# The edge table by exclusive-or and minimum, two groups of x instead of six, and the whole choice ahead of slots and running maxima

## The chip, the cores and the metric

The kernel runs on one core of one Trainium2 chip. The metric is device microseconds of one execution. The core has five engines that run side by side, each in its own program order: TensorE (PE in the profile; its weight loads are PEld), VectorE (DVE), ScalarE (ACT), GpSimd (POOL) and SyncE (SP). SP, ACT and POOL also issue DMA transfers; the gathers, whose row addresses lie in SBUF, are issued by POOL.

## The reference

The input is a graph: x has 6250 nodes of 256 features, and there are 100000 edges, sorted by their target node dst. Each node gets the maximum, over its incoming edges, of a linear map of both ends; then it is added to x and normalised.

```python
x_src = x[src]
x_dst = x[dst]
theta_x = (x_dst - x_src) @ theta_w.T + theta_b
phi_x = x_src @ phi_w.T + phi_b
e = jax.nn.relu(theta_x + phi_x)
out = jax.ops.segment_max(e, dst, num_segments=x.shape[0])
out = jnp.where(jnp.isfinite(out), out, 0.0)
x = _layernorm(x + out, axis=-1)
```

The part of an edge that depends on its source is b = x (phi_w - theta_w)^T, the rest depends on the target alone. So a node needs the maximum of the rows b[src] over its edges, and the target's own part is added afterwards.

## The kernel before

The first part of the nodes (1130) and the second (5120, 40 on each of 128 partitions) get their maxima in different ways.

**b.** All 49 row tiles of x (128 rows each) are loaded (x_q), transposed on TensorE (L746), copied by ScalarE (L748), multiplied by the weights (L758), copied again (L761) and stored to the DRAM tensor b_rows (L779). This is `b_of`.

**The first part.** Its edges lie 146 to a partition (`T1`), in 19 groups of 8 steps. A step is one gather of 128 rows by POOL (L512) into a tile of a ring of six (`gathered`, the tile g), and then one running maximum on VectorE (L688), each over the one before; a group's maxima are stored to maxima_1. A group that is gathered before b exists takes rows of x, and `x_group` runs `b_of` over them in place: `X_GROUPS` = 6 groups go this way, the rest gather from b_rows. Behind each gather, while `paced[0]` is 2, POOL runs two small iotas into a tile named pause.

**The second part** has two ways. For up to 24 edges of each node (`CHOICE_R`) nothing is gathered. The sources are cut into 17 slots of 383 nodes. For each slot, each node chooses one edge whose source lies in it (`choice`, nine batches of two slots, L1003 to L1021); the choice is transposed and sent to DRAM (`wanted`, chosen_rows). A part of the fetch (`slot_part`: one slot, 1024 nodes, 85 parts in all) loads the chosen rows' numbers (want, L1065), makes three blocks of one-hot columns from them (hot: two ScalarE instructions a block, L1071 and L1072, or, from the list on, one of VectorE, L1069, for the first of three blocks), and multiplies the slot's rows of b, split into a high and a low half (terms, L1057 and L1058), by them (L1079). VectorE takes the maximum into acc (L1090); for slot 0 ScalarE copies instead (L1088). The edges that no slot took form the list: `list_pieces` packs them on VectorE in 16 pieces (the moves are L1204 and L1207), sends them through DRAM, gathers them back in three long gathers (`gather_run`), and then 29 groups of 8 steps are gathered from b_rows by list_src and run as in the first part.

**The edge table** (`fill_table`) brings the edges of a partition's 40 nodes, up to 800 of them, from where they lie in order to a table of 40 x 36 places. Each word holds the distance that it has still to move, times WORD, and above zero its source; ten rounds (steps 512, 256, ... 1) move those whose bit is set. A round is three VectorE instructions: the moved words (L966), the words that stay (L969), and their sum (L972), between two tables in turn. A word of zero is an empty place.

**What sets the order.** A scheduler orders each engine's instructions by the order in the source and its own costs; `behind_in_order` pins one instruction behind another without a wait on the chip. `in_turn` keeps POOL's gathers in the order of the source, and each run's step is pinned behind a gather of the next group. In the list stage VectorE's runs are pinned behind the latest part's maximum (`latest_part`).

The order of the source is: gathers of x for six groups; b, with the first x group behind the seventh share and the others at the end; the table; nine times a choice, its `wanted` and `next_group_1(1)`; the list pieces, of which some carry `next_group_1(1)` and every other of the rest one part; what is left of the first part; the list's 29 groups, with the parts that are left spread over them; the closing shares (L1283 to L1348), which gather the maxima, add, normalise and store.

```python
def next_group_1(n):
    if groups_1:
        i = groups_1.pop(0)
        gathers = gather_group(i, b_rows)
        if i > X_GROUPS:
            run_1(i - 1, gathers)
    if todo:
        node_place(todo.pop(0))
    fetch_parts(n)
```

## Time and profile before

| what | us |
|---|---|
| median of three runs | 744.11 (743.1 to 745.2) |
| profiled execution, its time | 744.23 |
| its span on the core | 742.4 |
| TensorE busy | 655.6 |
| VectorE busy | 636.6 |
| ScalarE busy | 507.7 |
| GpSimd busy | 515.8 |

The profile is one execution. A group's row gives the source line, engine, operation, output and input tiles with their shapes, how often, the busy time in us with the mean of one in ns, and after the bar the time the engine was idle just before them, with what ended it. A row by stage gives start and end of a stretch, its length, the busy time of each engine with the number of its instructions, the clock granted to TensorE, the busy share of the DMA engines and GB/s. A row in order of time gives start, length, and what ran.

### The profile page before, as it was taken

The page shows a single profiled execution, that of the slowest core. Times are in us where ns is not written, and L with a number is a line of the kernel's source. Part 1 is how long each engine was busy: PE and PEld are TensorE (multiplying, and loading weights), DVE is VectorE, ACT ScalarE, POOL GpSimd, SP SyncE. Part 2 cuts the span into 40 slices and gives each one's busy share as a digit, 9 for nine tenths or more (in the row PEclk, how much of TensorE's full clock was granted, in tenths as well). Part 3 has the DMA queues.
Part 4 walks back from the last instruction along what each step waited for, and adds up shares of the span by engine and source line. Part 5 has one row for each costly group of instructions (what it writes and reads, how often), then busy time and mean ns, then how long its engine had stood idle before and what let it go on. Part 6 is the DMA issues. An engine that isn't in the chain of part 4 may idle for free.

```text
span 742.4 us, 10003 instructions
## 1 busy us (share of the span) xinstructions
PE 655.6 (88%) x3018; PEld 540.4 (73%) x3018; DVE 636.6 (86%) x1213; ACT 507.7 (68%) x714; POOL 515.8 (69%) x561
## 2 busy tenths in 40 slices
PE   0599998998875998899999999999999999789943
PEld 0388787886664866688888888888888888579943
DVE  6499999999987988498979888889888989968874
ACT  0144446969995797688778777877877776037882
POOL 7598987888987777777777777777767364037710
PEclk9999999999997899999999999999999999999986
DMA  7476756576477678988787878778867676336652
GB/s 219 135 254 207 274 192 221 167 255 205 139 228 231 215 215 300 300 295 271 235 264 221 283 250 248 242 240 284 269 209 244 186 255 208 137 107 192 206 200 76
DMA packets 56470, 164.83 MB, mean 222 GB/s; under 512 B 11899, under 2 KB 19860, under 8 KB 49332
## 3 DMA queue, kind: packets, MB, share of 16 engines
q1 hardware_dynamic: 32920, 98.76, 38.5%
q0 software_dynamic: 20944, 57.62, 27.3%
q10 hardware_dynamic: 2540, 7.69, 2.8%
q8 instruction: 27, 0.44, 0.3%
q14 instruction: 39, 0.32, 0.1%
HBM read 101.08 MB, written 63.74 MB: 222 GB/s over the span
## 4 chain that ended last, share of the span: by engine, by line
PE 49%; DVE 8%; POOL 7%; DMA 6%; ACT 6%; issue 4%; SPq 0%; DVEq 0%; ACTq 0%; POOLq 0%
PE ps_f L1079 45%; POOL g L512 6%; DMA g<-b_rows,src 4%; DMA want<-chosen_rows 2%; ACT x_f L1348 2%; ACT squares L1333 2%; PE ps_e L1303 2%; DVE acc L1090 2%; DVE g L688 1%; ACT x_t L1298 1%; DVE g L1314 1%; DVE x_f L1318 1%; PE ps_e L1296 1%; DVE work L1176 0%; POOL dst_w L512 0%
## 5 line engine op out<-in xcount | busy, mean ns | idle before, releaser
L1079 PE MATMUL ps_f<-hot,terms 128*128 128x512 f32 x1960 | 463.6, 397 | 30.7 <-DVE acc L1090 15.2
L1079 PEld LDWEIGHTS ps_f<-hot,terms 128*128 128x128 f32 x1960 | 371.9, 191 | 118.5 <-DVE acc L1090 18.5
L512 POOL DMA_INDIRECT g<-b_rows,list_src x232 | 233.2, 1005 | 84.6 <-issue 61.1
L1071 ACT ACTIVATE hot<-want,minus_row 128x1024 fp32r<-128x1024 f16 x179 | 197.4, 1146 | 82.6 <-PE ps_f L1079 72.6
L1090 DVE TENSOR_TENSOR acc<-acc,ps_f 128x1024 f32<-128x1024 f32 x160 | 193.4, 1215 | 30.5 <-PE ps_f L1079 29.6
L688 DVE SCALAR_TENSOR_TENSOR g<-g,caps 128x256 f32<-128x256 f32 x376 | 180.3, 479 | 15.2 <-DMA g<-b_rows,src 11.7
L1072 ACT ACTIVATE hot<-hot 128x1024 fp32r<-128x1024 f32 x179 | 179.5, 1047 | 0.0
L512 POOL DMA_INDIRECT g<-b_rows,src x98 | 130.4, 1330 | 30.0 <-issue 25.9
L758 PE MATMUL ps_b<-weights,x_t 128*128 128x256 f32 x388 | 92.4, 393 | 5.1 <-ACT x_t L748 4.5
L758 PEld LDWEIGHTS ps_b<-weights,x_t 128*128 128x128 f32 x388 | 74.0, 196 | 19.1 <-ACT x_t L748 9.3
L512 POOL DMA_INDIRECT g<-maxima,place x49 | 47.1, 962 | 54.6 <-DVE g L1315 29.2
L512 POOL DMA_INDIRECT g<-in_x_dram,src x48 | 62.5, 1302 | 11.6 <-issue 6.6
L1069 DVE TENSOR_SCALAR hot<-want,row_id 128x1024 fp32r<-128x1024 f16 x66 | 50.4, 766 | 6.7 <-DMA want<-chosen_rows 6.7
L1303 PE MATMUL ps_e<-weights,x_t 128*128 128x256 f32 x192 | 49.4, 386 | 0.2 <-ACT x_t L1298 0.2
L1303 PEld LDWEIGHTS ps_e<-weights,x_t 128*128 128x128 f32 x192 | 33.6, 195 | 3.8 <-ACT x_t L1298 0.5
L761 ACT COPY b_sb<-ps_b 128x512 f32<-128x512 f32 (+1 forms) x25 | 14.5, 578 | 29.1 <-PE ps_b L758 29.1
L1298 ACT COPY x_t<-ps_e 128x512 f32<-128x512 f32 x24 | 13.7, 575 | 29.6 <-PE ps_e L1296 29.6
L488 POOL IOTA pause<- 128x160 f32 x102 | 29.9, 293 | 3.4
L748 ACT COPY x_t<-ps_xt 128x512 f32<-128x512 f32 (+1 forms) x49 | 26.4, 594 | 6.1 <-PE ps_xt L746 5.9
L1333 ACT ACTIVATE squares<-x_f,r 128x256 bf16<-128x256 f32 x49 | 24.3, 500 | 7.7 <-DVE r L1330 7.7
L1348 ACT ACTIVATE x_f<-x_f,r 128x256 f32<-128x256 f32 x41 | 21.5, 591 | 9.2 <-DVE r L1340 9.1
L761 ACT COPY g<-ps_b 128x512 f32<-128x512 f32 x24 | 14.1, 589 | 17.8 <-PE ps_b L758 16.7
(267 smaller groups left out, 500.2 us busy)
## 6 DMA issues: line engine op xcount, KB each, us to landing
maxima<-g SPq DMA_DIRECT2D x47, 1024.0 KB
want<-chosen_rows SPq DMA_DIRECT2D x85, 256.0 KB
x_q<-in_x_dram SPq DMA_DIRECT2D x12, 512.0 KB
b_rows<-b_sb ACTq DMA_DIRECT2D x12, 512.0 KB
raw<-b_rows SPq DMA_DIRECT2D x16, 256.0 KB
x_f<-in_x_dram SPq DMA_DIRECT2D x4, 1024.0 KB
out_dram<-x_f SPq DMA_DIRECT2D x4, 1024.0 KB
g<-b_rows,list_src POOLq DMA_INDIRECT x232, 3.9
```

Source lines behind the costliest of these rows:

```text
L488: return nc.gpsimd.iota(t, pattern=[[step, t.shape[1]]], base=base, channel_multiplier=per_partition, allow_small_or_imprecise_dtypes=True,)
L512: in_turn(nc.gpsimd.indirect_dma_start(out=out, out_offset=out_offset, in_=in_, in_offset=in_offset))
L688: one = nc.vector.scalar_tensor_tensor(g[:, k, :], last[part], caps[:, t : t + 1], g[:, k, :], op0=ALU.min, op1=ALU.max)
L758: nc.tensor.matmul(ps[:, h, :], x_t[:, h, k, :], weights[:, k, 0, :], start=(k == 0), stop=(k == KC - 1))
L1069: nc.vector.tensor_scalar(hot[:, b, :], want, row_id[:, b : b + 1], None, op0=ALU.is_equal)
L1071: nc.scalar.activation(hot[:, b, :], want, AF.Abs, bias=minus_row[:, b : b + 1], scale=1.0)
L1072: nc.scalar.activation(hot[:, b, :], hot[:, b, :].bitcast(FP), AF.Relu, bias=1.0, scale=-1.0)
L1079: nc.tensor.matmul(ps[:, w : w + 512], terms[:, part, b, h * P : (h + 1) * P], hot[:, b, w : w + 512], start=(i == 0), stop=(i == n - 1),)
L1090: latest_part[0] = nc.vector.tensor_tensor(to, to, ps, op=ALU.max).ins.name
L1303: nc.tensor.matmul(a[:, i, :], x_t[:, 2 * i + c, :], weights[:, c, 1, :], start=(c == 0), stop=False)
L1333: nc.scalar.activation(squares, x_f[:, k, :], AF.Square, bias=mean[:, k : k + 1], scale=1.0, accum_out=var[:, k : k + 1])
L1348: nc.scalar.activation(x_f[:, k, :], x_f[:, k, :], AF.Identity, bias=mean[:, k : k + 1], scale=inv[:, k : k + 1])
```

## The change

- X_GROUPS goes from 6 to 2. Sixteen steps gather from x, the other 130 of the first part from b_rows. The two x groups get their `b_of` behind all shares, and their runs stand in the source behind the choices. The pauses behind the early gathers are gone.
- In the table, a word is a float between 2^23 and 2^24, whose low bits hold the source and above it the distance; an empty place is 2^100. A round is one exclusive-or with the step's bit on the words' bits, and one minimum into the same table: a word whose bit is set becomes smaller by it where it should go, and one whose bit isn't set becomes larger. The slot code is worked out after the spreading, over the whole table (`floor_of` on 1440 columns), instead of before it on 800. The list takes its sources out of the word by one mask.
- All nine choices come first; then two parts, the runs of the two x groups, and the list's 16 pieces, each with a `next_group_1` of one or two parts in turn. Eighteen gathers of the first part now stand on POOL behind the list's three long ones.
- `ahead_of_run` pins: slot 0's subtraction (L1058) behind the last choice, and the first running maximum of each first-part group behind the latest choice or list move. The memset of raw is pinned behind the table's words.

```diff
 FIRST_STEPS = 146
-X_GROUPS = 6
+X_GROUPS = 2
 TILES = 40
...
 CHOICE_R = 24
-X_AFTER = 6
-WORD = 8720
+WORD = 1 << 13
 TABLE_BITS = 10
...
 LOWEST = -1.0e30
-ABSENT = 1 << 14
+EMPTY = 2.0**100
+FAR_OFF = 2.0**30
 MAGIC = 12582912.0
...
     latest = [None]
-    paced = [2]
+    paced = [0]
...
     latest_part = [None]
+    ahead_of_run = [None]
...
                     behind_in_order(one, gathers[k], "rows that are there")
+                if part == 1 and k == 0 and ahead_of_run[0] is not None:
+                    behind_in_order(one, ahead_of_run[0], "choice and list ahead of the first part")
                 if part == 2 and latest_part[0] is not None:
...
                 b_of(rows, rows)
-            run_1(i)
-
-        for k, share in enumerate(shares(4)):
+
+        for share in shares(4):
             n = share[2]
...
             nc.scalar.dma_start(node_rows(b_rows, *share), present(b_sb, *share))
-            if k == X_AFTER:
-                x_group(of_x[0])
-        for i in of_x[1:]:
+        for i in of_x:
             x_group(i)
...
         source, w_3 = work_2[:, :W], work_1[:, TR - W :]
-        iota(w_3, 1, TR - W + 1, 0)
-        nc.vector.memset(words[:, : TR - W], 0.0)
-        nc.vector.memset(work_1[:, : TR - W], 0.0)
-        nc.vector.tensor_scalar(local, dst_w, first_node, None, op0=ALU.subtract)
+        iota(w_3, 1, TR - W + 1 + R // 2, 0)
+        nc.vector.memset(words[:, : TR - W], EMPTY)
+        nc.vector.tensor_scalar(local, dst_w, first_node, 0.5, op0=ALU.subtract, op1=ALU.add)
         valid = w_1
-        nc.vector.tensor_scalar(valid, local, 0.0, None, op0=ALU.is_ge)
+        nc.vector.tensor_scalar(valid, local, FAR_OFF, 1.0, op0=ALU.mult, op1=ALU.min)
         same = w_2
...
         nc.vector.tensor_tensor(distance, w_3, same, op=ALU.subtract)
-        nc.vector.tensor_copy(source, src_w)
-        slot = local
-        floor_of(slot, source, SLOT_ROWS)
-        nc.vector.tensor_scalar(source, source, 1.0, None, op0=ALU.add)
-        nc.vector.scalar_tensor_tensor(source, slot, float(SLOT - SLOT_ROWS), source, op0=ALU.mult, op1=ALU.add)
-        nc.vector.scalar_tensor_tensor(source, distance, float(WORD), source, op0=ALU.mult, op1=ALU.add)
-        nc.vector.tensor_tensor(words[:, TR - W :], source, valid, op=ALU.mult)
-        now, then, going = words, work_1, work_2
+        nc.vector.tensor_scalar(source, src_w, float(1 << 23), None, op0=ALU.add)
+        one = nc.vector.scalar_tensor_tensor(
+            words[:, TR - W :], distance, float(WORD), source, op0=ALU.mult, op1=ALU.add
+        )
+        behind_in_order(nc.vector.memset(raw, LOWEST), one.ins.name, "edge table ahead of a slot's rows")
+        going = work_2
         for i in reversed(range(TABLE_BITS)):
             step = 1 << i
-            first = TR - W if step >= TR - W - step else 0
-            a = max(first, step)
+            a = max(TR - W if step >= TR - W - step else 0, step)
             nc.vector.tensor_scalar(
-                going[:, a:], now[:, a:], float(-step * WORD), 0.0, op0=ALU.add, op1=ALU.max
+                going.bitcast(I32)[:, a:], words.bitcast(I32)[:, a:], step * WORD, None, op0=ALU.bitwise_xor
             )
-            nc.vector.scalar_tensor_tensor(
-                then[:, first:], now[:, first:], float(step * WORD), now[:, first:], op0=ALU.is_lt, op1=ALU.mult
-            )
-            nc.vector.tensor_tensor(
-                then[:, a - step : TR - step], then[:, a - step : TR - step], going[:, a:], op=ALU.add
-            )
-            now, then = then, now
-        assert now is words
-        nc.vector.tensor_scalar(work_1, words, 0.0, ABSENT + 1.0, op0=ALU.is_equal, op1=ALU.mult)
+            nc.vector.tensor_tensor(words[:, a - step : TR - step], words[:, a - step : TR - step], going[:, a:], op=ALU.min)
+        nc.vector.tensor_scalar(words, words, float(1 << 23), float(WORD - 1), op0=ALU.subtract, op1=ALU.min)
+        slot = work_1
+        floor_of(slot, words, SLOT_ROWS)
         nc.vector.scalar_tensor_tensor(
             padded.rearrange(by_rank, r=R),
+            slot.rearrange("p (j r) -> p r j", r=R),
+            float(SLOT - SLOT_ROWS),
             words.rearrange("p (j r) -> p r j", r=R),
-            -1.0,
-            work_1.rearrange("p (j r) -> p r j", r=R),
-            op0=ALU.add,
+            op0=ALU.mult,
             op1=ALU.add,
...
         for i in range(n):
-            nc.vector.tensor_tensor(unused[:, all_ranks], unused[:, all_ranks], in_slot[:, i, :], op=ALU.mult)
+            one = nc.vector.tensor_tensor(unused[:, all_ranks], unused[:, all_ranks], in_slot[:, i, :], op=ALU.mult)
+        ahead_of_run[0] = one.ins.name
...
     raw = slots.tile([P, KB, D], FP, name="raw", bufs=1)
-    nc.vector.memset(raw, LOWEST)
     terms_of = {}
...
         nc.scalar.copy(terms[:, 0, :n], raw[:, :n])
-        nc.vector.tensor_tensor(terms[:, 1, :n], raw[:, :n], terms[:, 0, :n].bitcast(FP), op=ALU.subtract)
+        one = nc.vector.tensor_tensor(terms[:, 1, :n], raw[:, :n], terms[:, 0, :n].bitcast(FP), op=ALU.subtract)
+        if s == 0:
+            behind_in_order(one, ahead_of_run[0], "choice ahead of the slots")
...
         left_over = wide_i16(3 * BATCH_S * CHOICE_R * TILES // 2, [P, TR])
-        nc.vector.scalar_tensor_tensor(left_over, padded, float(ABSENT), unused, op0=ALU.is_lt, op1=ALU.mult)
+        nc.vector.scalar_tensor_tensor(left_over, padded, float(SLOT * NS), unused, op0=ALU.is_lt, op1=ALU.mult)
         valid, count = work_1, work_2
...
             )
-            nc.vector.copy_predicated(done[:, :n], moves[:, :n], done[:, shift : shift + n])
+            one = nc.vector.copy_predicated(done[:, :n], moves[:, :n], done[:, shift : shift + n])
+            ahead_of_run[0] = one.ins.name
             yield
         nc.vector.tensor_scalar(done, done, (1 << 20) - 1, None, op0=ALU.bitwise_and)
-        nc.vector.tensor_tensor(done, done, owner.to_broadcast([P, OWN_LIST]), op=ALU.bitwise_or)
+        one = nc.vector.tensor_tensor(done, done, owner.to_broadcast([P, OWN_LIST]), op=ALU.bitwise_or)
+        ahead_of_run[0] = one.ins.name
         nc.sync.dma_start(flat(list_words, OWN_LIST, [[OWN_LIST, P], [1, OWN_LIST]]), done)
...
             nc.vector.copy_predicated(list_edges, mask, to)
-        key, slot = (t.bitcast(I32)[:, :LIST_CHUNK] for t in (wide[:, WINDOW : 2 * WINDOW], count))
-        nc.vector.tensor_scalar(key, list_edges[:, BACK:], (1 << 14) - 1, None, op0=ALU.bitwise_and)
-        nc.vector.tensor_scalar(key, key, -1, 0, op0=ALU.add, op1=ALU.max)
-        nc.vector.tensor_scalar(slot, key, SLOT_BITS, None, op0=ALU.logical_shift_right)
-        nc.vector.scalar_tensor_tensor(list_src, slot, SLOT_ROWS - SLOT, key, op0=ALU.mult, op1=ALU.add)
+        nc.vector.tensor_scalar(list_src, list_edges[:, BACK:], WORD - 1, None, op0=ALU.bitwise_and)
         nc.vector.tensor_scalar(list_src, list_src, N - 1, None, op0=ALU.min)
...
     fill_table()
-    paced[0] = 0
     for s0 in range(0, NS, BATCH_S):
         wanted(s0)
-        next_group_1(1)
+    fetch_parts(2)
+    for i in of_x:
+        run_1(i)
     chunk_heads()
     for i, _ in enumerate(list_pieces()):
-        if i in (3, 7, 14):
-            next_group_1(1)
-        else:
-            fetch_parts(i % 2)
-    next_group_1(1)
+        next_group_1(2 if i % 2 else 1)
     list_carry()
```

The assertions on sizes (WORD, the slot code) are changed to match and left out here.

More of the change, by code (lines that the diff above doesn't have):

```diff
@@ L446, in gnn_kernel @@
     NONE_1 = P * T1
+    slot_code = lambda i: i + i // SLOT_ROWS * (SLOT - SLOT_ROWS)
     assert D == 2 * P and LEFT1 > 0 and OWN % CW == 0 and TILES < 64 and P * T1 < E and WINDOW < E
     assert (P - 1) * T + 1 < E <= P * T and N < ID_MASK and P * T <= EDGES and E + 8 * P <= EDGES
-    assert SLOT * NS < min(ABSENT, WORD) and WORD << TABLE_BITS <= 1 << 24 and SLOT == 1 << SLOT_BITS and P == 1 << P_BITS and SLOT_ROWS < SLOT and KB == 3 and ROWS == P - 1 and WINDOW <= 8 * P and OWN_LIST * P < 1 << 20
+    assert SLOT * NS <= slot_code(WORD - 1) < 1 << 15 and N < WORD and WORD << TABLE_BITS == 1 << 23 and SLOT == 1 << SLOT_BITS and P == 1 << P_BITS and SLOT_ROWS < SLOT and KB == 3 and ROWS == P - 1 and WINDOW <= 8 * P and OWN_LIST * P < 1 << 20
     BATCH_S = 2
```

## The prediction

> **What bounds the kernel now.** I read the page's totals and chain first, then a table by stage, since the shares are averages.
>
> ```profile
> span 742.4 us, 10003 instructions
> PE 655.6 (88%) x3018; PEld 540.4 (73%) x3018; DVE 636.6 (86%) x1213; ACT 507.7 (68%) x714; POOL 515.8 (69%) x561
> ...
> PE ps_f L1079 45%; POOL g L512 6%; DMA g<-b_rows,src 4%; DMA want<-chosen_rows 2%; ACT x_f L1348 2%; ACT squares L1333 2%; PE ps_e L1303 2%; DVE acc L1090 2%; DVE g L688 1%; ACT x_t L1298 1%; DVE g L1314 1%; DVE x_f L1318 1%; PE ps_e L1296 1%; DVE work L1176 0%; POOL dst_w L512 0%
> ```
>
> The chain is the fetch matmuls (L1079) for nearly half the span, and ahead of them first-part gathers. The profiled execution took 744.23 us, 1.8 over its span, and 0.1 over the median of 744.11. The sum below moves its span and adds the 1.8.
>
> The busy time by stage:
>
> ```profile
> core 0: us, PE busy (x) PEld busy (x) DVE busy (x) ACT busy (x) POOL busy (x), PEclk, DMA share, GB/s
> 31.00:92.00 61.00, 58.59 (x302) 50.36 (x302) 60.41 (x77) 26.89 (x51) 53.87 (x82) 1.00 0.72 236
> 92.00:119.00 27.00, 25.75 (x136) 22.21 (x137) 26.10 (x60) 13.84 (x26) 23.90 (x42) 1.00 0.55 186
> 119.00:162.00 43.00, 40.32 (x200) 33.88 (x199) 41.38 (x109) 32.62 (x65) 33.75 (x30) 0.96 0.67 223
> 162.00:211.00 49.00, 40.09 (x159) 29.94 (x158) 49.00 (x71) 48.43 (x75) 43.20 (x21) 0.93 0.59 187
> 211.00:240.00 29.00, 19.53 (x73) 14.47 (x72) 22.19 (x56) 22.00 (x23) 22.44 (x23) 0.85 0.70 222
> ...
> 286.00:652.00 366.00, 354.53 (x1554) 290.39 (x1552) 317.49 (x471) 264.78 (x268) 245.38 (x245) 1.00 0.76 246
> 652.00:742.00 90.00, 68.72 (x416) 62.56 (x416) 63.66 (x233) 58.23 (x169) 38.11 (x40) 0.90 0.48 161
> ```
>
> Four stages follow from it. To about 119, TensorE makes b and VectorE makes the edge table and choices; both are full. From 119 to 286 lies phase 1: ScalarE and VectorE are full at 162 to 211, and all wait from 211 to 240. From 286 to 652 the list is gathered and TensorE is the bound (97% busy). The last 90 us are the closing shares, which the change doesn't touch.
>
> **The fetch by stage.** A part (one slot, 1024 nodes) is 24 matmuls; 80 such and 5 of 8 make 1960. The table by stage again, for L1079 alone (PE busy, PEld busy):
>
> ```profile
> 162.00:211.00 49.00, 38.35 (x144) 27.80 (x143) 0.93 0.59 187
> 211.00:240.00 29.00, 19.33 (x67) 13.71 (x66) 0.85 0.70 222
> 240.00:286.00 46.00, 43.46 (x176) 34.23 (x176) 0.94 0.73 220
> 286.00:317.00 31.00, 26.46 (x110) 19.49 (x109) 1.00 0.96 318
> 317.00:620.00 303.00, 303.00 (x1338) 250.91 (x1337) 1.00 0.77 247
> 620.00:652.00 32.00, 23.96 (x95) 18.26 (x94) 0.95 0.48 159
> ```
>
> Fed, TensorE needs 303/1338 = 0.226 us a matmul, 5.4 a part. From 162 to 286 it got 387 matmuls, 16.1 parts, in 124 us: 7.7 a part. All rows make 1930 of the 1960, so 30 came before 162.
>
> **The change, part by part. Four groups of x fewer.** Their 32 row tiles leave TensorE, and their 32 gathers move from x, at the start, to b_rows, after b.
>
> ```profile
> L758 PE MATMUL ps_b<-weights,x_t 128*128 128x256 f32 x226 | 53.0, 389 | 1.5 <-ACT x_t L748 1.2
> L746 PE MATMUL ps_xt<-ident,x_q 128*128 128x128 f32 x88 | 11.6, 273 | 0.0
> L746 PE MATMUL ps_xt<-ident,g 128*128 128x128 f32 x26 | 3.3, 273 | 0.0
> ...
> L761 ACT COPY b_sb<-ps_b x25: 373/586/599, 36.5 to 101.6; 128x512 f32<-128x512 f32 x24, 128x256 f32<-128x256 f32 x1
> ```
>
> The first three rows cover 36 to 102: 226 products at four to a tile are 56.5 tiles in 66 us, 1.17 each. So 32 tiles are 37 us less for TensorE. The first x group's 8 tiles stood inside b; moved behind, they let the last copy of b come at 101.6 - 9.4 = 92. I allow 4 us for its store, by the 4.26 us of a want load, the nearest transfer in the chain:
>
> ```profile
> 639.64 4.26 DMA want<-chosen_rows
> ```
>
> So b_rows is whole at 96. The 16 remaining tiles (19 us) end at 111. Dropping the two pauses behind each early gather is costed at nothing: the b stage covers them, since 48 such gathers with pauses ended before 119.9 (below), and 16 are left; without that cover they would be worth their own length on POOL.
>
> **The edge table.** Each of ten rounds loses its middle instruction (L969); exclusive-or and minimum stay as wide as the subtraction and addition were.
>
> ```profile
> L969 DVE SCALAR_TENSOR_TENSOR words<-work 128x1440 f32<-128x1440 f32 x5 | 8.2, 1649 | 0.0
> ...
> L969 DVE SCALAR_TENSOR_TENSOR work<-words 128x1440 f32<-128x1440 f32 (+1 forms) x5 | 7.6, 1514 | 0.0
> ...
> L960 DVE TENSOR_TENSOR words<-work,wide 128x800 f32<-128x800 f32 x1 | 1.0, 993 | 0.0
> ...
> L977 DVE TENSOR_SCALAR work<-words 128x1440 f32<-128x1440 f32 x1 | 0.9, 910 | 0.0
> ```
>
> That is 15.8 us. Six 800-wide ones go, at most 1.0 each like L960, some 4 net of the new conversion; the floor over 1440 adds two like L977, 1.8. Net 18. An integer exclusive-or and a float minimum aren't in this trace: between 0.9 us (L977) and 1.65 (L969) for either, I take 0.9 for the first, whose form is L977's, and 1.65 for the second; the ends are 7 us a kind apart over ten rounds. The smaller edits (raw's memset moved, four 232-wide instructions of the list's decoding gone) are under an L977 each, beside other work.
>
> **The whole choice first.** Nine choices, without a run or a subtraction of slot terms between. VectorE in order of time shows where three of them begin, and the page a run:
>
> ```profile
> 92.66 1.03 DVE L1003 TENSOR_SCALAR wide<-padded 128x960 int16<-128x960 int16 x2
> ...
> 100.78 0.74 DVE L1003 TENSOR_SCALAR wide<-padded 128x960 int16<-128x960 int16 x2
> ...
> 107.48 0.40 DVE L1003 TENSOR_SCALAR wide<-padded 128x960 int16<-128x960 int16 x1
> ...
> L688 DVE SCALAR_TENSOR_TENSOR g<-g,caps 128x256 f32<-128x256 f32 x376 | 180.3, 479 | 15.2 <-DMA g<-b_rows,src 11.7
> ```
>
> The second took 6.7 us with some 1.4 of other work in it (a run, a subtraction), so 5.3 each; eight and a half, since the last is of one slot: 45. They began at 92.7; minus 18, minus seven runs that stood ahead (3.4), at 71. They end at 116 to 117; slot 0's subtraction, now made to stand behind them, at 118. This is the added wait: behind it on VectorE stand the runs of two x groups (16 x 0.479, 7.7), and TensorE, which waits for it from 111 to 118. The first part starts near 119; before, 30 matmuls were done by 162. On SP the want loads of the first two parts stand ahead of those runs' stores, so they don't wait for them.
>
> **Phase 1** now issues 2 + 24 + 2 = 28 parts (19 before), 16 list pieces and 130 gathers (98 before).
>
> ```profile
> L1071 ACT ACTIVATE hot<-want,minus_row 128x1024 fp32r<-128x1024 f16 x179 | 197.4, 1146 | 82.6 <-PE ps_f L1079 72.6
> ...
> L1072 ACT ACTIVATE hot<-hot 128x1024 fp32r<-128x1024 f32 x179 | 179.5, 1047 | 0.0
> ```
>
> Three blocks of these two are 6.6 us a part, more than TensorE's 5.4, so ScalarE sets the pace; the measured 7.7 is the upper end. Two parts are prepared ahead, so part 28 ends between 119 + 26 x 6.6 = 291 and 319; I take 7.2, 306. Then 57 parts are left, 1288 matmuls, 291 us, with the losses of the before at both ends (4.5 in 286 to 317, 8 in 620 to 652): 610 against 652.
>
> **The gathers** are the other chain. The table by stage for POOL's L512 alone:
>
> ```profile
> 119.00:162.00 43.00, 33.53 (x29) 0.96 0.67 223
> 162.00:211.00 49.00, 43.09 (x20) 0.93 0.59 187
> ...
> 286.00:551.00 265.00, 202.93 (x202) 1.00 0.82 261
> ```
>
> Beside choices and runs one took 43/29 = 1.48 us, beside the list's moves 2.45, later 1.31. Before, 98 first-part gathers and the three of the list ran from 119.9 to 285.8 (POOL in order of time):
>
> ```profile
> 119.94 0.96 POOL L512 DMA_INDIRECT g<-b_rows,src  x1 [0.72 <-DMA maxima<-g]
> ...
> 267.61 0.94 POOL L512 DMA_INDIRECT dst_w<-list_words,run_start  x1 [1.32 <-DVE place_f L1167]
> ...
> 272.00 0.96 POOL L512 DMA_INDIRECT g<-b_rows,src  x1 [0.16 <-issue]
> ...
> 285.84 0.95 POOL L512 DMA_INDIRECT g<-b_rows,list_src  x1 [0.31 <-DVE carry_group L1253]
> ```
>
> The same 166 us and 32 more at 1.31 to 1.48 (45) from 96 on give 307 for the first list gather. 232 at 1.31 make 304, to 611; then two groups' runs, 7.7: 619. The later chain binds: 619 against 652, so 709.4 for the span and 711 for the time. Eighteen gathers (before, ten) stand behind the list's three on POOL: those took 4.4 us (267.6 to 272.0) and the ten 13.8, so eighteen take 25. They cover VectorE's last list work, which I cost at nothing; without them it would show at most the 13.8 that covered it before.
>
> The Trainium skill (SBUF — State Buffer, Who interferes with whom) says that a two-input VectorE instruction contends only with GpSimd work that reads SBUF, whereas copies and tensor_scalar in a two-port mode block descriptor writing. By it the choices, mostly two-input, would leave early gathers at 1.31 and save 3 us; the 2.45 beside the moves agrees with the second half.
>
> **The rivals.**
>
> ```profile
> L1069 DVE TENSOR_SCALAR hot<-want,row_id 128x1024 fp32r<-128x1024 f16 x66 | 50.4, 766 | 6.7 <-DMA want<-chosen_rows 6.7
> ```
>
> *VectorE stays the bound.* It is all but full to 211. It loses 18 us, and nine hot blocks of parts that are now issued before the list pass to ScalarE, 0.77 each, 7: 744 - 25 = 719. Against it: 49 of 366 us idle after 286. The Trainium skill (Perfetto Trace Analysis, Identifying the Most-Contended Engine) ranks TensorE by its weight loads, 73% here, below VectorE's 86%, and so points to this rival.
>
> *Phase 1 flows better.* Parts at 6.6 us, gathers at 1.48 throughout: 130 end at 288, list gathers start at 292 and end at 596, 604 with the runs; 48 us less, 696. TensorE's chain then ends earlier, at 291 + 291 + 12.
>
> *Slower: phase 1 locks up.* List pieces stand on VectorE behind maxima of parts; the three list gathers need the pieces, and 21 parts after the first two must be through. At r us a part the first list gather comes at 119 + 21r + 29, and the fetch ends 312 later. That equals 652 at r = 9.1. The row from 162 to 211 has 8.2, that from 211 to 240 has 10.4: at that, 678, and so 770. For it: all three engines of phase 1 are near full. Against: the mean of 7.7 had that stall in it.
>
> *Nothing comes of it:* r comes out near 9.1, 744.
>
> **How the numbers follow.** Forecast 0.56, its own range 702 (TensorE's 610 binds) to 720 (all 130 gathers at the old mean, 166/98 = 1.69); VectorE 0.18; better flow 0.13; slower 0.11; no change 0.02. A measurement of this kernel tells about 0.3%. Faster is 0.87, same 0.02, slower 0.11. The range goes from a little under the better flow, 693, to half way between VectorE's 719 and no change, 732; the slower case, no change and the far ends of the others stay out.
>
> **What would show it.** After: last b copy near 92, table done near 72, last choice near 117, first fetch matmul near 119, first list gather near 307, TensorE full from there, closing shares near 619 and unchanged in length. The forecast is wrong if the list gathers start past 335, or if TensorE shows waits for VectorE's maxima in the list stage.

## The result

The changed kernel takes 764.59 us (median, 761.87 to 772.37), the kernel before 744.65 beside it: 1.0275 of before, 95% interval 1.0204 to 1.0346. It is slower; 711 was forecast. The profiled execution took 772.37 us, 1.8 over its span; it is the slowest of this kernel's executions, and the same kernel's second profile (e7 below) took 756.8.

The totals of the page after, and its table by stage (columns as before; the last stage is the closing one, 90 us long as before):

```profile
span 770.6 us, 9428 instructions
PE 625.0 (81%) x2826; PEld 510.8 (66%) x2826; DVE 615.6 (80%) x1187; ACT 508.4 (66%) x700; POOL 483.1 (63%) x465
```

```profile
core 0: us, PE busy (x) PEld busy (x) DVE busy (x) ACT busy (x) POOL busy (x), PEclk, DMA share, GB/s
...
162.00:211.00 49.00, 43.01 (x180) 32.89 (x181) 45.49 (x75) 49.00 (x72) 42.60 (x22) 1.00 0.57 189
211.00:240.00 29.00, 20.65 (x73) 15.57 (x71) 19.07 (x52) 20.97 (x26) 22.30 (x23) 0.82 0.69 222
240.00:286.00 46.00, 1.33 (x3) 0.50 (x2) 2.23 (x4) 7.01 (x7) 35.00 (x39) 0.53 0.43 125
286.00:320.00 34.00, 28.59 (x111) 22.37 (x112) 30.86 (x65) 19.66 (x20) 21.91 (x23) 0.88 0.87 301
...
680.00:770.00 90.00, 68.76 (x416) 62.52 (x414) 64.38 (x235) 58.20 (x169) 38.07 (x40) 0.90 0.48 161
```

TensorE, VectorE and POOL have less work than before, ScalarE as much, and the span is 28.2 us longer. From 240 to 286 TensorE, VectorE and ScalarE all but stand still (1.3, 2.2 and 7.0 us busy of 46) and only POOL works. The longest waits name the place:

```profile
ACT hot L1065 <- DMA want<-chosen_rows: 61.4, 7, 48.6
...
PE ps_f L1073 <- DVE acc L1084: 51.6, 4, 43.3
DVE dst_w L1222 <- DMA dst_w<-list_words,run_start: 42.0, 1, 42.0
```

VectorE waits once, 42.0 us, ahead of the first instruction that decodes the list (L1222; before, 2.4 us in all). The fetch's maxima (L1084) stand behind it, and TensorE waits 43.3 us for those. Three engines in order of time show what it waits for: VectorE, then POOL, then SyncE's queue.

```profile
244.37 1.00 DVE L690 SCALAR_TENSOR_TENSOR g<-g,caps 128x256 f32<-128x256 f32 x2
287.38 0.46 DVE L1222 COPY_PREDICATED dst_w<-words,dst_w 128x266 int32<-128x266 int32 x1 [42.01 <-DMA dst_w<-list_words,run_start]
```

```profile
246.83 0.95 POOL L513 DMA_INDIRECT g<-b_rows,src  x1 [0.30 <-issue]
248.08 0.94 POOL L513 DMA_INDIRECT g<-b_rows,src  x1 [0.30 <-issue]
...
281.84 0.94 POOL L513 DMA_INDIRECT g<-b_rows,src  x1 [0.30 <-issue]
283.09 0.95 POOL L513 DMA_INDIRECT dst_w<-list_words,run_start  x1 [0.30 <-issue]
```

```profile
206.07 2.45 SPq L1210 DMA_DIRECT2D list_words<-work  x1
```

The list's words were sent at 206. POOL reached the first of the three gathers that fetch them (L513, dst_w) only at 283, because first-part gathers stand ahead of it in its queue, one each 1.25 us. In the written order VectorE's decoding stands behind 93 of the first part's 145 running maxima (its first step needs none), POOL's three gathers behind 128 of its 146 gathers: 35 between them, at 1.25 us 44.

Before the wait, the changed kernel was ahead. By 245 us the fetch (L1073) had begun 363 matmuls, before (L1079) 259. Then, for the fetch alone (PE busy, clock, DMA), first the kernel before and behind it the changed one:

```profile
245.00:288.00 43.00, 40.46 (x174) 0.99 0.71 222
```

```profile
245.00:288.00 43.00, 0.73 (x2) 0.50 0.39 113
```

The lead of 104 matmuls, 24 us, is gone in one wait.

### The profile page after: what moved, and what is told of

Read it like the earlier page. It is cut to its first block, busy times and chain, and to the rows that moved or that the text cites. A ratio compares the mean times of both kernels' runs of the same rounds, so it can differ in the third digit from the quotient of the medians.

```text
span 770.6 us, 9428 instructions
## 1 busy us (share of the span) xinstructions
PE 625.0 (81%) x2826; PEld 510.8 (66%) x2826; DVE 615.6 (80%) x1187; ACT 508.4 (66%) x700; POOL 483.1 (63%) x465
## 4 chain that ended last, share of the span: by engine, by line
PE 39%; ACT 14%; DVE 9%; DMA 9%; POOL 6%; issue 6%; DVEq 0%; POOLq 0%; ACTq 0%; SPq 0%
PE ps_f L1073 36%; POOL g L513 6%; ACT hot L1065 5%; DMA want<-chosen_rows 4%; ACT hot L1066 3%; DMA g<-b_rows,src 3%; ACT x_f L1340 2%; ACT squares L1325 2%; PE ps_e L1295 2%; DVE acc L1084 2%; DVE g L690 2%; DMA g<-b_rows,list_src 1%; ACT x_t L1290 1%; DVE x_f L1310 1%; DVE g L1306 1%
## 5 line engine op out<-in xcount | busy, mean ns | idle before, releaser
L1073 PE MATMUL ps_f<-hot,terms 128*128 128x512 f32 x1960 | 469.8, 400 | 81.5 <-DVE acc L1084 51.6
L1073 PEld LDWEIGHTS ps_f<-hot,terms 128*128 128x128 f32 x1960 | 374.2, 193 | 173.7 <-DVE acc L1084 54.8
L513 POOL DMA_INDIRECT g<-b_rows,list_src x232 | 233.7, 1007 | 88.2 <-issue 61.4
L1065 ACT ACTIVATE hot<-want,minus_row 128x1024 fp32r<-128x1024 f16 x188 | 207.4, 1149 | 123.1 <-PE ps_f L1073 61.7
L513 POOL DMA_INDIRECT g<-b_rows,src x130 | 168.7, 1298 | 93.2 <-DMA want<-chosen_rows 54.2
L1084 DVE TENSOR_TENSOR acc<-acc,ps_f 128x1024 f32<-128x1024 f32 x160 | 192.9, 1215 | 35.8 <-PE ps_f L1073 35.0
L1066 ACT ACTIVATE hot<-hot 128x1024 fp32r<-128x1024 f32 x188 | 188.9, 1050 | 0.0
L513 POOL DMA_INDIRECT g<-maxima,place x49 | 47.2, 962 | 34.7 <-DMA maxima<-g 20.1
L762 PE MATMUL ps_b<-weights,x_t 128*128 128x256 f32 x260 | 60.0, 385 | 0.7 <-ACT x_t L752 0.4
L762 PEld LDWEIGHTS ps_b<-weights,x_t 128*128 128x128 f32 x260 | 48.8, 192 | 8.5 <-ACT x_t L752 2.3
L1063 DVE TENSOR_SCALAR hot<-want,row_id 128x1024 fp32r<-128x1024 f16 x57 | 43.1, 757 | 0.0
L1222 DVE COPY_PREDICATED dst_w<-words,dst_w 128x266 int32<-128x266 int32 x2 | 0.9, 454 | 42.0 <-DMA dst_w<-list_words,run_start 42.0
L765 ACT COPY b_sb<-ps_b 128x512 f32<-128x512 f32 (+1 forms) x25 | 14.5, 579 | 25.5 <-PE ps_b L762 25.5
L1340 ACT ACTIVATE x_f<-x_f,r 128x256 f32<-128x256 f32 x41 | 21.5, 590 | 9.0 <-DVE r L1332 9.0
L513 POOL DMA_INDIRECT g<-in_x_dram,src x16 | 18.2, 1140 | 9.7 <-issue 7.2
L1288 PE MATMUL ps_e<-ident,x_f 128*128 128x128 f32 x96 | 14.8, 280 | 11.0 <-DVE r L424 9.2
L1298 PE MATMUL ps_e<-bias_terms,pick 128*128 128x256 f32 x48 | 22.7, 474 | 0.0
```

The costliest lines, as they stand in the source:

```text
L513: in_turn(nc.gpsimd.indirect_dma_start(out=out, out_offset=out_offset, in_=in_, in_offset=in_offset))
L762: nc.tensor.matmul(ps[:, h, :], x_t[:, h, k, :], weights[:, k, 0, :], start=(k == 0), stop=(k == KC - 1))
L1063: nc.vector.tensor_scalar(hot[:, b, :], want, row_id[:, b : b + 1], None, op0=ALU.is_equal)
L1065: nc.scalar.activation(hot[:, b, :], want, AF.Abs, bias=minus_row[:, b : b + 1], scale=1.0)
L1066: nc.scalar.activation(hot[:, b, :], hot[:, b, :].bitcast(FP), AF.Relu, bias=1.0, scale=-1.0)
L1073: nc.tensor.matmul(ps[:, w : w + 512], terms[:, part, b, h * P : (h + 1) * P], hot[:, b, w : w + 512], start=(i == 0), stop=(i == n - 1),)
```

## The experiments

Theory A: VectorE's written order puts the decoding ahead of what POOL has ready, and the wait is the loss. Rival B: the row of 128 gathers on POOL is the bound wherever VectorE waits. Later two more came up, for the pace of the fetch beside the first part: D, the loads of the wanted rows stand on SyncE's queue behind stores that wait for runs; E, VectorE's written order of runs and maxima.

On the chips of the runs e1 to e4 and e13 to e16 the kernel before took 922 and 908 us; no trace shows why. e1 to e4 took 962, 963, 1020 and 948 us there. These times are not compared with the others; of these chips' runs only the wait ahead of the decoding is read, in e1 and e2.

**The decoding behind the runs whose gathers stand ahead of the list's (e1, e5).**

```diff
+                if part == 1:
+                    latest_run[0] = one.ins.name
...
-            nc.vector.copy_predicated(list_edges, mask, to)
+            one = nc.vector.copy_predicated(list_edges, mask, to)
+            if to is second:
+                behind_in_order(one, latest_run[0], "runs ahead of the list's words")
```

> The changed kernel with one pin more: VectorE's first conditional copy of the list's decoding stands in program order behind the last run of the fifteenth group (128 runs ahead of it instead of 93). Theory A (VectorE waits in program order, 42 us, for a gather that POOL reaches 35 gathers later): the wait of that copy falls under 6 us, the fetch goes on through 245 to 288, and the time is 728 to 738. Theory B (POOL's row of 130 gathers is the bound whatever VectorE does): the same 40 us come back as waits of the runs for their gathers, 755 or more.

> The same edit as in the first run of this edit: the list's decoding on VectorE stands behind the first-part runs whose gathers stand ahead of the list's on POOL. Theory A (VectorE's program order holds the fetch up): the 42 us wait ahead of the decoding's first instruction is gone, the fetch gets at least 100 matmuls between 245 and 288 us instead of 2, and the kernel is 20 to 35 us faster than the changed one, at 0.975 to 1.00 of the kernel before. Theory B (128 gathers ahead of the list's three on POOL are the bound, wherever VectorE waits): within 8 us of the changed kernel, 1.02 to 1.035 of the kernel before; the wait shows again as POOL's wait for the decoding ahead of the first list gather, 20 us or more.

In both the 42 us wait is gone. e5 took 746.64 us, 1.0008 of before (0.9969 to 1.0047), the changed kernel on the same chip (e7) 762.98, 1.024 (1.0182 to 1.0297):

> The changed kernel, as the measure for the other runs of this chip. Both theories: 1.02 to 1.035 of the kernel before, with a wait of 38 to 46 us ahead of the decoding's first instruction.

So the order carries 16.3 us. That is under A's 20, and its ratio just misses A's range, but the fetch got 114 matmuls between 245 and 288, as A asked, and B's "within 8 us" falls. In e7 the wait was 40.1. Of e5, the stage from 245 to 288 (all engines), its waits from 119 to 370, and SyncE's waits from 119 to 320 (before, the same row has 29.4):

```profile
245.00:288.00 43.00, 32.54 (x114) 24.73 (x112) 24.97 (x43) 24.86 (x25) 33.21 (x37) 0.84 0.74 242
```

```profile
DVE g L691 <- DMA g<-b_rows,src: 32.9, 12, 4.4
...
ACT hot L1068 <- DMA want<-chosen_rows: 24.7, 6, 5.2
```

```profile
SPq L703 <- DVE g L691: 73.7, 11, 11.9
```

The wait is gone and TensorE works again, but three quarters of the time only; shorter waits, 12 us at most, stand where the long one was.

**The list's gathers earlier on POOL, alone (e2) and with the decoding matched to them (e6).**

```diff
-        next_group_1(2 if i % 2 else 1)
+        if i % 3 != 2:
+            next_group_1(1)
+        else:
+            fetch_parts(1)
```

> The changed kernel with fewer first-part groups between the list pieces (two pieces in three), so that the three list gathers stand on POOL behind 96 first-part gathers instead of 128; on VectorE the scheduler puts the decoding behind 76 runs. Theory A: the wait is what POOL still has to issue, (96 - 76) x 1.25 = 25 us at most, less what POOL is ahead; about 15 to 25 us instead of 42, and the time 742 to 757. Theory B: the first list gather doesn't move, and neither does the time, 760 to 768.

> Both at once: one group of the first part a piece less, so that the list's three gathers stand behind 96 first-part gathers on POOL instead of 128, and the decoding behind 87 runs on VectorE. Theory A: no wait of more than 10 us ahead of the decoding; 25 to 45 us faster than the changed kernel, 0.965 to 0.995 of the kernel before. Theory B: with 50 first-part gathers left behind the list's three the first list gather starts no sooner than in the changed kernel (316), and the time is within 10 us of the changed kernel, 1.015 to 1.04 of the kernel before.

e2 has 96 gathers ahead and 76 runs: its wait was 20.5 us. e6 has 96 and 87; its time is 741.59 us, 0.9939 of before (0.9903 to 0.9976), and 21.4 us under the changed kernel (A had said 25 to 45). Against before the gain is clear of noise but only 0.6%. Its wait and the list's gathers:

```profile
DVE dst_w L1225 <- DMA dst_w<-list_words,run_start: 8.1, 1, 8.1
```

```profile
L513 POOL DMA_INDIRECT dst_w<-list_words,run_start x3: 949/959/963, 233.3 to 236.1; - x3
```

The wait goes with the count of gathers ahead of the list's three on POOL, less the runs ahead of the decoding on VectorE, at 1.25 us each. All orders of the other chips, and e2 (e8 to e12, e17 and e18 are told below):

| kernel | gathers | runs | difference x 1.25 | wait measured |
|---|---|---|---|---|
| changed | 128 | 93 | 43.8 | 42.0 and 40.1 |
| e2 | 96 | 76 | 25.0 | 20.5 |
| e17 | 136 | 119 | 21.3 | 14.5 |
| e6 | 96 | 87 | 11.3 | 8.1 |
| e10 | 96 | 87 | 11.3 | 12.9 |
| e18 | 96 | 87 | 11.3 | none listed |
| e8 | 136 | 128 | 10.0 | 5.5 |
| before | 136 | 128 | 10.0 | 2.4 |
| e9 | 136 | 129 | 8.8 | 2.8 |
| e12 | 104 | 98 | 7.5 | 0.7 |
| e11 | 136 | 131 | 6.3 | 4.1 |
| e5 | 128 | 127 | 1.3 | none listed |

But for e18 the wait lies between 1.6 us above the product and 8 below. In e18 the order holds VectorE's runs back behind the fetch: it reached the decoding only at 291, when the words were there. So the product tells about how long the wait can get, and VectorE's own delay takes from it. That the order makes the long wait is shown by e5, which moved the decoding alone and lost it.

**The parts of the change alone.** Two groups of x in the kernel before (e3, e12), and the new table in the order of before with six groups (e4, e8; of the change's pins only raw's memset stays):

```diff
-X_GROUPS = 6
+X_GROUPS = 2
```

> The kernel before with two groups of x instead of six and nothing else. Theory A: here the list gathers stand behind 112 first-part gathers and the decoding behind 98 runs, so a wait of up to 17 us appears; TensorE is relieved of 37 us; 728 to 748. Theory B (the 32 gathers moved behind b are what makes the change slower): 755 or more.

> Two x groups alone, with the table and the order of before. Theory A (only an order that puts the decoding ahead of its gathers costs): no decoding wait above 5 us, 0.985 to 1.01 of before. Theory D: TensorE loses 37 us of work ahead of 119, but the 32 more gathers from b hold the stores and, behind them, the loads of the wanted rows: 1.01 to 1.05, with over 60 us of SyncE's waits for runs from 119 to 320.

```diff
-X_GROUPS = 2
+X_GROUPS = 6
...
-    fetch_parts(2)
-    for i in of_x:
-        run_1(i)
+        next_group_1(1)
...
-        next_group_1(2 if i % 2 else 1)
+        if i in (3, 7, 14):
+            next_group_1(1)
+        else:
+            fetch_parts(i % 2)
+    next_group_1(1)
```

> The kernel before with the new edge table and nothing else: VectorE's table and the choices end 18 us earlier by the prediction's sum; the decoding stays behind 128 runs. If VectorE is the bound to the end of the runs, 726 to 730; if POOL's gathers and TensorE's b set the pace as in theory A, 736 to 744.

> The new edge table alone, with six x groups and the order of before. Theory A: no decoding wait above 5 us; the table's 18 us on VectorE come ahead of the choices, and 5 to 18 us of them reach the end: 0.975 to 0.995 of the kernel before. Theory B (the gathers of the first part are the bound in any case): 0.995 to 1.005 of it. If the table itself is what costs, 1.01 to 1.04.

e12 took 764.26 us, 1.0277 (1.0183 to 1.0371), e8 766.98, 1.026 (1.0207 to 1.0314): each part alone is as slow as both, though neither has the long wait. A's ranges missed both, and for e8 the range put down to the table itself came; D's for e12 held, with 57.8 us of SyncE's waits for runs, a little under the 60 it asked for. For e12 the trace shows what reads as the same fault the other way round, though no edit tested it: the stage from 245 to 288, POOL's wait, and the list's gathers from b.

```profile
245.00:288.00 43.00, 39.98 (x162) 31.76 (x161) 39.05 (x69) 39.86 (x41) 5.73 (x8) 0.92 0.28 87
```

```profile
POOL dst_w L512 <- DVE apart L1161: 37.4, 1, 37.4
```

```profile
L512 POOL DMA_INDIRECT g<-b_rows,list_src x232: 945/949/1515, 343.0 to 651.9; - x116
```

Here POOL stands 37.4 us ahead of the list's three gathers, waiting for places that VectorE has not computed, with 42 first-part gathers queued behind; the list's gathers from b start at 343 instead of 286.

For all kernels but e9 to e11, the fetch begun by 364 us, from where TensorE is full, tells the end as long as the gathers aren't later still (0.226 us a matmul; spans against before; each count is of one window from 0, while those in the expectations are sums over several and count some matmuls twice):

| kernel | list gathers from b | matmuls by 364 | against before, us | span against before |
|---|---|---|---|---|
| before | 285.8 to 608.0 | 737 | | |
| changed | 316.3 to 655.1 | 632 | +23.7 | +28.2 |
| e7 | 303.1 to 640.9 | 692 | +10.2 | +12.5 |
| e5 | 306.0 to 629.7 | 742 | -1.1 | +2.7 |
| e6 | 303.3 to 634.7 | 765 | -6.3 | -5.4 |
| e12 | 343.0 to 651.9 | 663 | +16.7 | +24.1 |
| e8 | 286.7 to 635.0 | 618 | +26.9 | +27.7 |
| e17 (below) | 283.9 to 632.7 | 631 | +24.0 | +26.5 |
| e18 (below) | 342.7 to 686.8 | 883 | -33.0 | +52.2 |

So the table alone loses its time before 364, in a fetch beside list gathers that start when they did before. SyncE's queue in order of time shows a pattern there:

```profile
242.06 0.32 SPq L701 DMA_DIRECT2D maxima<-g  x1
242.48 2.12 SPq L1061 DMA_DIRECT2D want<-chosen_rows  x2
255.40 0.32 SPq L701 DMA_DIRECT2D maxima<-g  x1
257.73 1.43 SPq L1049 DMA_DIRECT2D raw<-b_rows  x3
259.26 0.34 SPq L1061 DMA_DIRECT2D want<-chosen_rows  x1
264.85 0.34 SPq L701 DMA_DIRECT2D maxima<-g  x1
```

A store of first-part maxima waits for its runs, and the loads of the wanted rows go out right behind it: theory D.

**The loads of the wanted rows on ScalarE's queue**, with the table alone (e9), with the earlier list (e10), and in the kernel before as control (e11):

```diff
-        nc.sync.dma_start(want, flat(chosen_rows, s * OWN + c * CW, [[0, P], [1, CW]]))
+        nc.scalar.dma_start(want, flat(chosen_rows, s * OWN + c * CW, [[0, P], [1, CW]]))
```

> The table-alone kernel (770.1 us of span, 27.7 over before; its fetch is 121 matmuls behind at 364 us), with the loads of the wanted rows moved from SyncE's queue to ScalarE's. Theory D: SyncE sends the stores of the first part and the loads of the wanted rows in one order, and the stores wait for runs that wait for gathers (99.5 us of such waits from 119 to 320, before 29.4), so the fetch gets about one part for each group of 8 gathers. Then 15 to 28 us come back: 0.985 to 1.005 of before, and ScalarE's 28.1 us of waits for these loads fall under 10. Theory E: the sums of the fetch stand on VectorE behind the runs that wait for gathers, and that alone sets the pace. Then within 6 us of the table-alone kernel: 1.018 to 1.034, with VectorE's 27 us of waits for gathers kept.

> The changed kernel with the decoding and the list's gathers earlier (0.994 of before), and the loads of the wanted rows on ScalarE's queue. Theory D: its 15.2 us of ScalarE's waits for these loads mostly go: 0.975 to 0.99 of before. Theory E: within 4 us of the kernel without the move: 0.989 to 1.0.

> The control: the kernel before, with the loads of the wanted rows on ScalarE's queue. Before, ScalarE waited 10.1 us for these loads from 119 to 370. Theory D: 0.985 to 1.0. Theory E: 0.995 to 1.005. Over 1.01 would mean that the move has a cost of its own on ScalarE, which the two runs beside it then carry too.

e9 took 781.82 us, 1.0528 (1.0436 to 1.062), e10 797.98, 1.0736 (1.0644 to 1.0828), and the control 769.75, 1.0356 (1.0265 to 1.0446). The move costs more in the control than it could give, so it does not tell D and E apart. ScalarE's waits for these loads fell from 28.1 us to 13.1 in e9, and no time came back.

**The first part's runs ordered behind the fetch**, with the table alone (e13, e17) and, with the earlier list, at one (e14) or two parts a group (e15, e18), and in the kernel before (e16):

```diff
+                if part == 1 and k == 0 and latest_part[0] is not None:
+                    behind_in_order(one, latest_part[0], "fetch ahead of the first part")
```

> The table alone (1.026 of before), with the first run of each first-part group ordered on VectorE behind the latest of the fetch's maxima issued before it. In VectorE's written order the table-alone kernel has 16 of the fetch's maxima ahead of run 144 of the first part, the kernel before 25, this kernel 29; a part has two, so the 9 missing are 4.5 parts, 108 matmuls at 0.226 us, 24 us. Theory E (the order that is planned for VectorE in the first part's stage, no engine and no queue, carries the loss): 0.99 to 1.008 of before, and the fetch no more than 30 matmuls behind before at 364 us (table alone: 121). Theory D (the loads of the wanted rows behind the stores on SyncE): within 8 us of the table-alone kernel, 1.015 to 1.035, with over 20 us of ScalarE's waits for these loads.

> The changed kernel with decoding and list gathers earlier (0.994 of before; 34 of the fetch's maxima ahead of run 144), and the same order of runs behind the fetch: 50 ahead of run 144. Theory E: up to 8 parts more of the fetch beside the first part, less what ScalarE's 6.6 to 7.7 us a part allow from 211 to 317: 0.965 to 0.99 of before, with the fetch over 50 matmuls ahead of before at 364 us. Against it: the runs are held, so the ring comes free later and the list's gathers start later; if that decides, 0.995 to 1.02, and TensorE is not full from 364.

> As the run before, with two parts of the fetch for each first-part group: 72 of the maxima ahead of run 144. A group of 8 gathers is 10 us alone, two parts are 13 to 15 us of ScalarE, so the first part ends 18 groups times 3 to 5 us later at the most. Theory E: TensorE fuller ahead of 317, 0.955 to 0.99 of before. If the first part's delay decides: the first list gather past 350 us and 0.99 to 1.03.

> The control: the kernel before with the same order, 28 of the fetch's maxima ahead of run 144 (25 without). Theory E: 0.985 to 1.003. Over 1.01 would mean that the order has a cost of its own.

> The table alone with the first-part runs ordered behind the fetch's maxima, once more. Theory E (VectorE's planned order carries the table-alone kernel's loss of 2.6%): 0.99 to 1.008 of before, the fetch no more than 30 matmuls behind before at 364 us. Theory D (SyncE's queue): 1.015 to 1.035, ScalarE still waits over 20 us for the wanted rows' loads.

> The changed kernel with decoding and list gathers earlier, runs behind the fetch, two parts a group, once more. Theory E: 0.955 to 0.99 of before, TensorE fuller ahead of 317 us. If the delay of the first part decides: first list gather past 350 us, 0.99 to 1.03.

On their chip e13 to e16 took 941, 938, 926 and 907 us beside 908: no order among them can be read. On another chip e17 took 769.03, 1.029 (1.0212 to 1.0368), outside E's 0.99 to 1.008, and its fetch was 106 matmuls behind at 364. But this does not refute E, because the edit brought a wait of its own. The fetch alone up to 260 us (columns as from 245 to 288), in the kernel before, in e8 and in e17, and then e17's wait:

```profile
0.00:260.00 260.00, 86.67 (x324) 0.95 0.66 210
...
0.00:260.00 260.00, 68.64 (x242) 0.92 0.63 204
...
0.00:260.00 260.00, 77.99 (x287) 0.94 0.64 207
...
DVE dst_w L1226 <- DMA dst_w<-list_words,run_start: 15.0, 2, 14.5
```

With more maxima ahead on VectorE the fetch was 37 matmuls behind before at 260, not 82 as in e8. Then the held runs left the decoding waiting for 14.5 us (136 gathers against 119 runs), and at 275 the fetch was 95 behind, as in e8. Nor did the edit change what stands ahead of the decoding: 12 of the fetch's maxima in e8 and in e17, 20 in the kernel before. Slot 0's five parts need no maximum there and every later part needs two. When the decoding began, 380 matmuls were issued in the kernel before, 292 in e8 and in e17, 334 in e11 (16 maxima) and 261 in e9 (10). These counts fit E, but no run moved that order without moving something else.

e18 took 797.5, 1.0702 (1.0629 to 1.0775), outside both ranges of its expectation. Its stage from 245 to 288, and its list gathers:

```profile
245.00:288.00 43.00, 40.15 (x166) 30.10 (x165) 28.72 (x44) 43.00 (x53) 22.52 (x23) 1.00 0.62 193
```

```profile
L513 POOL DMA_INDIRECT g<-b_rows,list_src x232: 942/946/1812, 342.7 to 686.8; - x116
```

With two parts a group ScalarE is full, the fetch is 146 matmuls ahead of before at 364, and it is of no use: the first part's gathers come late, the list's gathers start at 343 and end 79 us later than before, and they set the end. The fetch and the first part share this stage; what one gains there the other loses. Why the table alone slows the fetch stays open: the counts above point to VectorE's order, and no experiment has shown it.

## Why the prediction was wrong

Two steps failed. They make most of the 53.6 us between 711 and 764.59.

The one that made the kernel slower than before is the sentence on the list's gathers: "Eighteen gathers (before, ten) stand behind the list's three on POOL ... They cover VectorE's last list work, which I cost at nothing; without them it would show at most the 13.8". I counted what stands behind the three, and never what stands ahead of them on POOL against what stands ahead of their reader on VectorE. 128 against 93 made a wait of 42 us, with everything queued behind the reader waiting too. In time it carries 16.3 us: 762.98 (e7) less 746.64 (e5).

The other is a term that was mis-sized, and it is the larger: "I take 7.2, 306" for 28 parts. Without the long wait (e5) the fetch had 527 matmuls by 306, 22.0 parts, 8.5 us a part from 119 on. Six parts at 5.4 us are 32 us: 709.4 + 32 is 741, against e5's span of 745.1. So without the wait the change would have gained nothing. 741 + 16.3 is 758, against 762.8 for the median less 1.8; the rest is open. ScalarE's busy time was right (L1065 and L1066 take 1149 and 1050 ns), but it was not what set the pace: in e5 it waits 24.7 us for wanted rows and VectorE 32.9 for gathers. I had dropped the measured 7.7, and the 10.4 of 211 to 240, as one stall of the order before. The written order would have told: in e5 33 of the fetch's maxima, 16.5 parts, stand ahead of VectorE's 144th first-part run, with slot 0's five 21.5, and that run came at 312. e18, with 72 ahead of it, had 27.7 parts by 306, but its first list gather came at 343. The forecast asked for both at 306 and 307, and no order here gave both.

The other steps, by the trace after:

- *b and its gathers*: last copy of b at 92.7 (forecast 92), first gather from b at 97.1 (96). Right.
- *The table*: two terms were chosen between ends, 0.9 and 1.65 us, and measured 0.847 and 1.536; the first choice begins at 71.8 (forecast 71). Right.

```profile
L966 DVE TENSOR_TENSOR words<-words,work 128x800 f32<-128x800 f32 (+9 forms) x10 | 15.4, 1536 | 0.3
...
L963 DVE TENSOR_SCALAR work<-words 128x800 int32<-128x800 int32 (+9 forms) x10 | 8.5, 847 | 0.2
```

- *The choices*: done at 122.7, not 116 to 117, and slot 0's subtraction at 122.6, not 118. Seven runs of the first x group stand between the choices: the new order acts on a group's first step, and the very first step issues no instruction. All but six of the fetch's matmuls came from 123.6 on, not 119.
- *The early gathers*: the first 14 from b took 97.1 to 120.3, 1.66 us each beside choices, and from 119 to 162 one took 43/22 = 1.95, with the list's moves among VectorE's work. My 1.48 was too low for both. POOL's busy time on L513:

```profile
92.00:119.00 27.00, 17.94 (x14) 0.96 0.49 143
119.00:162.00 43.00, 35.76 (x22) 0.87 0.54 175
```

  The Trainium skill (SBUF — State Buffer, Who interferes with whom) had two-input VectorE instructions leave descriptor writing alone. The price of 1.31 that I worked out by it was further off than my own: beside the choices a gather was busy for 17.94/14 = 1.28 us, and 0.30 us passed between two.
- *The first list gather*: forecast 307; 306.0 without the wait (e5), 316.3 and 303.1 (e7) with it. The sum was right up to there, partly by luck: the early gathers were slower than priced. The 232 list gathers then took 325 us in e5, not 304, and 322 in the kernel before: the 1.31 came from a row that ends at 551. In e5 the fetch ended last (653), not the gathers.
- *The rivals*: the slower one gave 770, close to the 764.59, but by another mechanism: pieces that wait for maxima of parts. The pieces were through by 206. Its pace, 10.3 us a part from 119 to 316 with 19.1 parts done, came about through the one wait on top of e5's 8.5. I gave it 0.11, too little for a stage in which four queues wait for one another.
- *The signs*: "if the list gathers start past 335, or if TensorE shows waits for VectorE's maxima in the list stage". Neither came: 316, and the 43.3 us wait for maxima lies ahead of the list stage. The signs watched the two ends of the chain and not the crossing in its middle.

## What to carry to other kernels

Where an in-order engine reads what another in-order queue delivers, count what stands ahead of the reader on its engine and ahead of the delivery on its queue, in the same units of work: the difference times the spacing of the queue is about the longest wait that the order can make, and everything behind the reader pays it. Read the written order for that, since a change elsewhere can move one of the two; here the whole change broke such a crossing on VectorE's side, and two x groups alone, by the trace, on POOL's. Read from the same order how many parts of one job can be through before a given step of the other: a price per part alone put 28 where the order had 21.5. A lead in one stage is worth something only if no queue that the next stage needs was held back for it (e18).

## What the runs showed that was not expected

TensorE's granted clock fell to 0.53 in the 46 us in which it stood still, and was 0.88 in the 34 us after, although it was 84% busy there; in the kernel before it was 1.00 from 286 to 652. What that cost is not shown: from 288 to 317 the clock was 0.71 in e5, which has no long wait, and 1.00 in e7, which has one.

The same kernel with the same wait lost twice as much in one profile as in the other: its fetch was 105 matmuls behind before at 364 in the first and 45 in e7. In the first POOL issued 22 first-part gathers from 162 to 211, in e7 31, and everything behind them came some 13 us later. So two profiles, one of each kernel, can put 10 or 25 us of span on one wait, and the medians, 16.3, are what counts.

Moving 85 loads of 256 KB from SyncE's queue to ScalarE's cost 25 us in the kernel before (e11), and VectorE's written order changed with it: 16 of the fetch's maxima ahead of the decoding instead of 20. One moved DMA is not an experiment on that DMA alone when the order is planned anew.
